# A four-layer graph kernel: adjacency tiles fetched up to 16 uses ahead, x in another queue, layer 2 counted before it is weighed, layer 3's side chains spread between its operations

## The chip, the cores and the metric

The kernel runs on one core of one Trainium2 chip. The metric is the device time in microseconds (us). Most executions of a kernel agree within about 1%. Stage times are read from one profiled execution per kernel, in microseconds from its first instruction. The granted clock of a profile is the share of its full clock that TensorE was given.

## The reference, cut to what matters

```python
# x: 3327 x 64, adj: 3327 x 3327 (sparse values in a dense float32 matrix)
h = relu(layernorm(x)); x = x + L0(h, adj)   # two gated products adj @ (h @ W)
h = relu(layernorm(x)); x = x + L1(h, adj)   # adj @ logmap0(h), then norms, tanh, projection
h = relu(layernorm(x)); x = x + L2(h, adj)   # rank of each nonzero in its row, weights 2**-k
h = relu(layernorm(x)); x = x + L3(h, adj)   # all pairs: distance, sigmoid attention * adj, sum
```

Every layer needs the whole adjacency matrix, 44 MB, and layer 0 needs it twice. It doesn't fit on the chip, so tiles are fetched again and again: 52 tiles (26 row blocks of 128 by two column groups of 12 and 14 blocks), 260 uses in a fixed order. The groups are named by their pairs of blocks: a "6-block" tile is 128x1536, a "7-block" tile 128x1792.

## The kernel before

The order of the 260 uses is known when the kernel is built. A small planner decides at build time which tile is loaded into which of the slots (16 in layers 0 and 1, 7 in layer 2, 4 in layer 3), and after which use:

```python
AHEAD = 5
...
    def ahead(self):
        for u in range(self.now, min(self.now + AHEAD, len(self.uses))):
            key = self.uses[u]
            if any(k == key and s < self.limit(u) for s, (k, _) in self.slots.items()):
                continue                      # it is there already
            wanted = set(self.uses[self.now : u + 1])
            able = [s for s, (k, _) in self.slots.items() if s < self.limit(u) and k not in wanted]
            if not able:
                break
            s = max(able, key=lambda s: self.next_use(s, self.now))   # farthest next use goes
            self.slots[s] = (key, self.load(s, key))
```

Tile loads are issued by SyncE (`nc.sync`). x, the weights and the biases are issued by ScalarE (`S`), in front of its first activation:

```python
    for ca, cb in starts:
        S.dma_start(xn[:, 2 * ca : 2 * cb, :], t["x"][:, 2 * ca : 2 * cb, :])
    ...
    # for each of two gate sets: three weights, two halves each, then two biases
    G.memset(w, 0.0)
    S.dma_start(w[h * D : (h + 1) * D, :, h * D : (h + 1) * D], ...)
    S.dma_start(b[:, 0, :], t["bih" + n])
    S.dma_start(b[:, 1, :], t["bhh" + n])
```

Work that isn't the main stream of an engine (gates, norms, the preparation of the next layer) is written as generators. `weave.tick()` lets each of them go on by one step, `weave.until(g)` runs one to its end. The order of the built instructions follows from where the ticks stand. Every engine executes its own list in that order.

Layer 2, per tile: VectorE makes a 0/1 mask, TensorE counts nonzeros with two triangular 128x128 matrices, ScalarE turns counts into weights, TensorE weighs:

```python
            mask(n + 2)
            for k in range(2):
                count(n, k)                                  # 128x128 matmuls
                flush(n, 2 if len(todo) > 2 * LAG else 1)    # weighing: 64-column matmuls
                weave.tick()
            todo += [(n, 0), (n, 1)]
```

Layer 3 is a software pipeline over 26 pairs of blocks. One iteration ends with a block of side work, and after the 13th pair a check of a bound stands in TensorE's own stream:

```python
            if n >= 0:
                gather_p(n)
                if n % HB == HB - 1:
                    collect(g)                     # evict, transpose, scale: all at once
                    final = weave.add(finish(g))
            for _ in range(6):
                weave.tick()
            if n == HB - 1:
                T.transpose(p[:2, :P], least, ident)
                V.tensor_reduce(leastr, p[:2, :P], axis=AX.X, op=OP.min)
                T.transpose(p[:1, P : P + 2], leastr, ident[:2, :2])
                ...
```

GpSimd fills three buffers of layer 3 with zeros while layer 1 ends, and the preparation of layer 3 ends with 13 small transfers that ScalarE issues, once in layer 2 and once in layer 3:

```python
    G.memset(rows_j, 0.0)          # 128 x 3328 bf16
    G.memset(rows_i, 0.0)
    G.memset(p2c, 0.0)
    ...
        for i in (6, 0, 1, 2, 3, 4, 5):
            if i == 6:
                S.dma_start(rows_l[:, ts]..., src); continue
            for lo in (0, D):
                S.dma_start(rows[r0 : r0 + 3, ts]..., src)
```

Of the kernel before, what the change touches and what calls it, by code (L numbers as in the profile page):

```python
# [43 lines left out]
AHEAD = 5  # L44
# [73 lines left out]
class Stream:  # L118
# [31 lines left out]
    def ahead(self):  # L150
        for u in range(self.now, min(self.now + AHEAD, len(self.uses))):
# [9 lines left out]
            s = max(able, key=lambda s: self.next_use(s, self.now))  # L161
            self.slots[s] = (key, self.load(s, key))

    def tile(self, key):

        assert self.uses[self.now] == key
        return next(
            a for s, (k, a) in self.slots.items() if k == key and s < self.limit(self.now)
        )
# [12 lines left out]
def gnn_kernel(ctx: ExitStack, tc: tile.TileContext, t, out):  # L182
# [27 lines left out]
    for ca, cb in starts:  # L210
        S.dma_start(xn[:, 2 * ca : 2 * cb, :], t["x"][:, 2 * ca : 2 * cb, :])
# [224 lines left out]
    def run(tg, acc, sources, m, ready, first, last):  # L436

        for i, k in enumerate(sources):
# [5 lines left out]
                stream.tile((tg, k)),  # L444
# [279 lines left out]
    def nodes3(g, m_t):  # L724
# [103 lines left out]
        yield 5  # L828
# [12 lines left out]
    with ExitStack() as c2:  # L841
# [20 lines left out]
        def mask(n):  # L862
            if n < len(work):
                a = stream.tile(work[n])
                g = GROUPS[work[n][0]]
                masks[n] = mk.tile([P, WIDE], BF16, name="mask", tag="mask", bufs=4)
                V.tensor_scalar(masks[n][:, : 2 * g.w], a, 0.0, None, op0=OP.not_equal)  # L867
                stream.done()
# [55 lines left out]
        def flush(n, most):  # L924
            while todo and most and todo[0][0] <= n - LAG:
                gens = need[work[todo[0][0]][1]]
                if weave.runs(*gens):
                    if len(todo) < 2 * (WB - 1):
# [12 lines left out]
        for n in range(len(work)):  # L941
            mask(n + 2)
            for k in range(2):
                count(n, k)
                flush(n, 2 if len(todo) > 2 * LAG else 1)
                weave.tick()
            todo += [(n, 0), (n, 1)]
        flush(len(work) + LAG, len(todo))
# [96 lines left out]
    with ExitStack() as cf:  # L1045
# [67 lines left out]
        def weights(n):  # L1113

            i, c = pairs[n]
            for b in range(2):
                a = stream.tile((i, 2 * c + b))
# [47 lines left out]
        def collect(g):  # L1165
            m = big(g, "h_n")
            m = flat(m)
# [5 lines left out]
            pp = flat(big(g, "xc"))  # L1173
# [4 lines left out]
            for p, k in each(natural(g, m)):  # L1178
                V.tensor_mul(
                    sums[:, g.slots, :D][:, k, :], p, bc(qs[:, g.slots][:, k])  # L1180
                )
            ((p, _, _),) = pieces(1)
            n0, n1 = m0 // P, m1 // P
# [9 lines left out]
            for q, n in enumerate((n0, n1)):  # L1193
# [5 lines left out]
                )  # L1199



        for n in range(-2, len(pairs)):
            if n + 2 < len(pairs) and pairs[n + 2] == (1, 0):
                weave.until(gen_s)
            if n >= 0:
                products3(n)
            if 0 <= n + 1 < len(pairs):
                distances(n + 1, 1)
            if n >= 0:  # L1210
                gather(n)
            if 0 <= n + 1 < len(pairs):
                weights(n + 1)
                squares(n + 1)
            if n + 2 < len(pairs):
                begin(n + 2)
                distances(n + 2, 0)
            if n >= 0:
                gather_p(n)
                if n % HB == HB - 1:  # L1220
                    g = GROUPS[pairs[n][0]]
                    collect(g)
                    final = weave.add(finish(g))
            for _ in range(6):
                weave.tick()
            if n == HB - 1:

                p = bank(1)
                T.transpose(p[:2, :P], least, ident)
                leastr = n3.tile([2, 1], F32, name="leastr")  # L1230
                V.tensor_reduce(leastr, p[:2, :P], axis=AX.X, op=OP.min)
                T.transpose(p[:1, P : P + 2], leastr, ident[:2, :2])
                leastr = n3.tile([1, 1], F32, name="leastr1")
                V.tensor_reduce(leastr, p[:1, P : P + 2], axis=AX.X, op=OP.min)
                within = n3.tile([1, 1], I32, name="within")
                V.tensor_scalar(within, leastr, X2_LEAST, None, op0=OP.is_ge)
            if n == HB + 1:
                ok = nc.values_load(within, min_val=0, max_val=1)
        weave.until(final)
    c3.close()  # L1240
# [223 lines left out]
```

## Time and profile before

| | before |
|---|---|
| time | 891.08 us median of 3 runs (886.57 to 892.96) |
| profiled execution | 892.6 us from the first to the last instruction |
| busy | PE 711.7 us (80%), DVE 457.2 (51%), ACT 402.8 (45%), POOL 9.7 (1%) |
| tile loads | 224, of 768 or 896 KB |

No engine is at its limit over the whole span, so the average says little. The prediction below cuts the span into stages and shows those lines. The timeline of ScalarE at the start; the columns are start, busy time, engine, line, operation, count, and in brackets the idle time before with what ended it:

```profile
32.88 1.28 ACT L468 ACT_TABLE_LOAD   x1 [32.88 <-DMA adj<-in_adj]
```

ScalarE computes nothing for 32.88 us: its list begins with transfers, and it stands behind them. Second, two timelines of layer 1's last run, VectorE and then GpSimd:

```profile
355.13 0.24 DVE L543 TENSOR_SCALAR z<-un,sc 128x14 f32<-128x14 f32 x1
356.24 0.17 DVE L633 TENSOR_SCALAR un<-un 128x14 f32<-128x14 f32 x1
```

### The profile page before, as it was taken

The numbers are of one execution on the slowest core, as the hardware profiler recorded it, in microseconds if no ns is written. First come the engines' busy times: TensorE is split into PE (matmuls) and PEld (weight loads), VectorE is DVE, ScalarE is ACT, GpSimd is POOL, SyncE is SP. The second block draws the span as 40 slices with busy tenths as digits, with TensorE's granted clock in tenths as the row PEclk, the third lists the DMA queues.
The fourth block names the chain that finished last, engine by engine and source line by source line (L and its number), as shares of the span: only waits on it lengthen the run. The fifth ranks groups of instructions, "written<-read, shape, count | busy, mean of one in ns | idle before, by whom it ended". The sixth has DMA issues, their size and how long they took to land.

```text
span 892.6 us, 10060 instructions
## 1 busy us (share of the span) xinstructions
PE 711.7 (80%) x4021; PEld 290.1 (33%) x4032; DVE 457.2 (51%) x743; ACT 402.8 (45%) x451; POOL 9.7 (1%) x20
## 2 busy tenths in 40 slices
PE   0297998989889878579998769568599995699980
PEld 0142433323334222234334324322234442244430
DVE  0230300202715402674336722488499997889976
ACT  0110200101202102176666546765599993699951
POOL 1000000000000000300000000000000000000000
PEclk9999999999999999899999979869699996799986
DMA  8819994098870999967776644123246551445600
GB/s 300 292 38 396 420 417 189 1 383 347 312 288 8 402 419 419 386 234 276 263 253 208 239 152 155 43 103 105 86 169 220 190 169 62 139 160 199 205 9 21
DMA packets 37563, 193.57 MB, mean 217 GB/s; under 512 B 7941, under 2 KB 8453, under 8 KB 37509
## 3 DMA queue, kind: packets, MB, share of 16 engines
q1 hardware_dynamic: 32544, 191.18, 56.9%
q10 hardware_dynamic: 4964, 1.68, 0.8%
q8 instruction: 33, 0.54, 0.2%
q14 instruction: 22, 0.17, 0.1%
HBM read 191.73 MB, written 0.85 MB: 216 GB/s over the span
## 4 chain that ended last, share of the span: by engine, by line
PE 51%; DMA 26%; DVE 12%; ACT 6%; issue 2%; ACTq 1%; POOL 1%; SPq 0%; DVEq 0%
DMA adj<-in_adj 23%; PE bank L428 9%; PE pair L1064 9%; PE bank L1140 9%; PE bank L916 6%; PE pair L882 4%; PE bank L1157 4%; PE pair L890 4%; PE pair L1076 2%; DVE gl L1128 1%; ACT th L1091 1%; ACT gl L1084 1%; PE pair L507 1%; PE pair L510 1%; DMA w<-in_W 1%
## 5 line engine op out<-in xcount | busy, mean ns | idle before, releaser
L428 PE MATMUL bank<-adj,m_a 128*64 128x384 f32 (+1 forms) x832 | 162.5, 527 | 25.2 <-DMA adj<-in_adj 24.4
L898 ACT ACTIVATE w<-pair,ebias 128x896 uint16<-128x896 f32 (+1 forms) x104 | 98.4, 952 | 62.1 <-PE pair L890 41.8
L1064 PE MATMUL pair<-xs 64*128 64x384 f32 x208 | 101.7, 571 | 15.7 <-ACT gl L1084 15.7
L1119 DVE SCALAR_TENSOR_TENSOR th<-th,adj 128x1792 f32<-128x1792 f32 (+1 forms) x52 | 97.8, 1886 | 21.3 <-ACT th L1091 20.9
L1084 ACT ACTIVATE gl<-pair 128x896 f32<-128x896 f32 (+1 forms) x104 | 84.1, 862 | 46.9 <-PE pair L1076 34.0
L1140 PE MATMUL bank<-gl,xd 128*64 128x384 f32 (+1 forms) x416 | 90.9, 582 | 17.3 <-DVE gl L1128 17.3
L1064 PE MATMUL pair<-xw,xs 64*128 64x384 f32 x208 | 101.4, 569 | 0.0
L1128 DVE SCALAR_TENSOR_TENSOR gl<-gl,th 128x1792 f32<-128x1792 f32 (+5 forms) x78 | 97.6, 1305 | 0.0
L428 PEld LDWEIGHTS bank<-adj,m_a 128*64 128x64 f32 x832 | 54.4, 138 | 125.7 <-DMA adj<-in_adj 65.0
L428 PE MATMUL bank<-adj,m_b 128*64 128x384 f32 (+1 forms) x416 | 81.2, 529 | 10.0 <-DMA adj<-in_adj 10.0
L1091 ACT ACTIVATE th<-leftb,righth 128x1792 f32<-128x1792 f32 (+1 forms) x52 | 87.7, 1687 | 0.0
L867 DVE TENSOR_SCALAR mask<-adj 128x1792 bf16<-128x1792 f32 (+1 forms) x52 | 52.9, 1022 | 63.5 <-PE pair L882 57.4
L421 DVE COPY m_t<-bank 128x384 f32<-128x384 f32 x6 | 3.3, 556 | 157.9 <-PE bank L428 157.9
L419 ACT ACTIVATE m_t<-bank 128x384 f32<-128x384 f32 (+1 forms) x6 | 3.3, 544 | 172.9 <-PE bank L428 172.9
L882 PE MATMUL pair<-mask,rest 128*128 128x384 bf16 (+1 forms) x190 | 65.7, 346 | 18.4 <-ACT w L898 18.3
L890 PE MATMUL pair<-mask,tri 128*128 128x384 bf16 (+1 forms) x207 | 70.7, 344 | 7.1 <-DVE mask L867 6.6
L916 PE MATMUL bank<-w,m_b 128*64 128x384 bf16 (+1 forms) x416 | 57.0, 354 | 0.0
L1140 PEld LDWEIGHTS bank<-gl,xd 128*64 128x64 f32 x416 | 33.2, 151 | 69.1 <-DVE gl L1128 37.2
L1064 PEld LDWEIGHTS pair<-xs 64*128 64x128 f32 x208 | 35.6, 197 | 43.1 <-issue 22.0
L1076 PE MATMUL pair<-rows_i,rows_j 64*128 64x384 bf16 x208 | 49.4, 353 | 0.0
L428 PEld LDWEIGHTS bank<-adj,m_b 128*64 128x64 f32 x416 | 27.7, 139 | 61.7 <-issue 32.2
L1157 PE MATMUL bank<-gl,p2c 128*32 128x384 f32 (+1 forms) x416 | 44.5, 519 | 0.0
(274 smaller groups left out, 665.1 us busy)
## 6 DMA issues: line engine op xcount, KB each, us to landing
adj<-in_adj SPq DMA_DIRECT2D x108, 896.0 KB
adj<-in_adj SPq DMA_DIRECT2D x116, 768.0 KB
xn<-in_x ACTq DMA_DIRECT2D x3, 192.0 KB
out<-h_n SPq DMA_DIRECT2D x1, 448.0 KB
out<-h_n SPq DMA_DIRECT2D x1, 384.0 KB
xn<-in_x ACTq DMA_DIRECT2D x1, 256.0 KB
ih<-in_wihT ACTq DMA_DIRECT2D x4, 48.0 KB
hh<-in_whhT ACTq DMA_DIRECT2D x4, 48.0 KB
```

Source lines behind the costliest of these rows:

```text
L428: T.matmul(acc[q][h * D : (h + 1) * D, : hi - lo], lhsT=m[:, k, :], rhs=a[:, h * g.w + lo : h * g.w + hi], start=first, stop=last,)
L882: T.matmul(dst, lhsT=rest, rhs=masks[n - 1][:, cs], start=False, stop=False, skip_group_check=True,)
L890: T.matmul(dst, lhsT=tri, rhs=masks[n][:, cs], start=first, stop=True, skip_group_check=True,)
L898: S.activation(ws[n][:, h * g.w : (h + 1) * g.w], cnt[h][:, P : P + g.w], AF.Relu, bias=ebias, scale=-EXP_UNIT,)
L916: T.matmul(acc2[i][q][h * D : (h + 1) * D, : hi - lo], lhsT=p[:, k, :], rhs=ws[n][:, h * g.w + lo : h * g.w + hi].bitcast(BF16), start=n % ...
L1064: T.matmul(pts[b][:, P + lo : P + hi], lhsT=xs[rs, c * P : (c + 1) * P], rhs=rhs[rs, g.c0 * P + lo : g.c0 * P + hi], start=True, stop=False,)
L1084: S.activation(gl[n][b][:, k * g.w : (k + 1) * g.w], pts[b][:, P : P + g.w], AF.Gelu, scale=-HA,)
L1091: S.activation(ths[n][k][:, : 2 * g.w], leftb[:, g.off : g.off + 2 * g.w], AF.Tanh, bias=righth[:, kk : kk + 1], scale=0.5,)
L1119: V.scalar_tensor_tensor(th, th, 1.0, a, op0=OP.add, op1=OP.mult)
L1128: V.scalar_tensor_tensor(a, a, hd, th[b][:, lo:hi], op0=OP.add, op1=OP.mult)
L1140: T.matmul(acc["x"][q][k * D : (k + 1) * D, : hi - lo], lhsT=xd[:, 2 * c + b, :], rhs=gl[n][b][:, k * g.w + lo : k * g.w + hi], start=firs ...
L1157: T.matmul(acc["p"][r : r + 32, : hi - lo], lhsT=p2c[:, 2 * c + b, :], rhs=a[b][:, k * g.w + lo : k * g.w + hi], start=first, stop=last,)
```

## The change

The intent: keep the transfers busy where they stood idle, bring x first, save TensorE's changes between two kinds of matmul in layer 2, and fill the idle holes of layer 3 by spreading side work. The diff, cut to its core (line numbers of the changed kernel are 2 to 4 higher):

```diff
-AHEAD = 5
+AHEAD = 16
@@ ahead()
             s = max(able, key=lambda s: self.next_use(s, self.now))
+            if self.next_use(s, self.now) < u:
+                break
             self.slots[s] = (key, self.load(s, key))
@@ x
-        S.dma_start(xn[:, 2 * ca : 2 * cb, :], ...)
+        nc.sync.dma_start(xn[:, 2 * ca : 2 * cb, :], ...)
@@ layer 2 (a tile also stays in its slot two uses longer: stream.done() moved out of mask())
-            for k in range(2):
-                count(n, k)
-                flush(n, 2 if len(todo) > 2 * LAG else 1)
-                weave.tick()
+            stream.done()
+            count(n, 0)
+            weave.tick()
+            count(n, 1)
             todo += [(n, 0), (n, 1)]
+            flush(n, 4 if len(todo) > 2 * LAG + 2 else 2)
+            weave.tick()
@@ layer 3: six single ticks, after products3, distances, weights, squares, distances and at the end
-            for _ in range(6):
-                weave.tick()
@@ layer 3: collect() split into evict() and a generator collected(), one pair later
+                if n == HB:
+                    final = weave.add(collected(gf, *evict(gf)))
@@ layer 3: the bound's check becomes a generator, started before the turn
-            if n == HB - 1:
-                ... transposes and reductions in a row ...
+                gen_b = weave.add(bound(), 4)
@@ the preparation of layer 3 waits for its rows longer
-        yield 5
+        yield 12
```

More of the change, by code (lines that the diff above doesn't have):

```diff
@@ L161, in ahead, with tile @@
             s = max(able, key=lambda s: self.next_use(s, self.now))
+            if self.next_use(s, self.now) < u:
+                break
             self.slots[s] = (key, self.load(s, key))
-    def tile(self, key):
-        assert self.uses[self.now] == key
+    def tile(self, u):
         return next(
-            a for s, (k, a) in self.slots.items() if k == key and s < self.limit(self.now)
+            a
+            for s, (k, a) in self.slots.items()
+            if k == self.uses[u] and s < self.limit(u)
         )
@@ L210, in gnn_kernel @@
     for ca, cb in starts:
-        S.dma_start(xn[:, 2 * ca : 2 * cb, :], t["x"][:, 2 * ca : 2 * cb, :])
+        nc.sync.dma_start(xn[:, 2 * ca : 2 * cb, :], t["x"][:, 2 * ca : 2 * cb, :])
     WIDE = 2 * max(g.w for g in GROUPS)
@@ L443, in run @@
                 k,
-                stream.tile((tg, k)),
+                stream.tile(stream.now),
                 m,
@@ L863, in mask @@
             if n < len(work):
-                a = stream.tile(work[n])
+                a = stream.tile(stream.starts[1] + n)
                 g = GROUPS[work[n][0]]
@@ L867, in mask @@
                 V.tensor_scalar(masks[n][:, : 2 * g.w], a, 0.0, None, op0=OP.not_equal)
-                stream.done()
         def count(n, h):
@@ L927, in flush @@
                 if weave.runs(*gens):
-                    if len(todo) < 2 * (WB - 1):
+                    if len(todo) < 2 * WB:
                         return
@@ L1116, in weights @@
             for b in range(2):
-                a = stream.tile((i, 2 * c + b))
+                a = stream.tile(stream.now)
                 th = ths[n][b][:, : 2 * GROUPS[i].w]
@@ L1163, in gather_p, with evict @@
                         )
-        def collect(g):
-            m = big(g, "h_n")
-            m = flat(m)
+        def evict(g):
+            m, pp = flat(big(g, "h_n")), flat(big(g, "xc"))
             for q, (lo, hi) in enumerate(g.chunks):
@@ L1172, in collect @@
                     V.tensor_copy(m[:, lo:hi], acc["x"][q][:, : hi - lo])
-            pp = flat(big(g, "xc"))
             m0, m1 = (hi - lo for lo, hi in g.chunks)
@@ L1177, in collect, with collected @@
                 S.activation(pp[D:, m0:m1], acc["p"][D:, m0:m1], AF.Copy)
-            for p, k in each(natural(g, m)):
-                V.tensor_mul(
-                    sums[:, g.slots, :D][:, k, :], p, bc(qs[:, g.slots][:, k])
-                )
+            return m, pp
+        def collected(g, m, pp):
+            yield
+            n0, n1 = ((hi - lo) // P for lo, hi in g.chunks)
             ((p, _, _),) = pieces(1)
-            n0, n1 = m0 // P, m1 // P
             for i in range(n1):
@@ L1199, in collect, with bound @@
                 )
+            yield
+            for p, k in each(natural(g, m)):
+                V.tensor_mul(sums[:, g.slots, :D][:, k, :], p, bc(qs[:, g.slots][:, k]))
+                yield
+            yield from finish(g)
+        def bound():
+            p = bank(1)
+            T.transpose(p[:2, :P], least, ident)
+            low = n3.tile([2, 1], F32, name="low")
+            V.tensor_reduce(low, p[:2, :P], axis=AX.X, op=OP.min)
+            yield 2
+            p = bank(1)
+            T.transpose(p[:1, :2], low, ident[:2, :2])
+            low = n3.tile([1, 1], F32, name="lowest")
+            V.tensor_reduce(low, p[:1, :2], axis=AX.X, op=OP.min)
+            V.tensor_scalar(within, low, X2_LEAST, None, op0=OP.is_ge)
+            yield
+        within = n3.tile([1, 1], I32, name="within")
+        final = None
         for n in range(-2, len(pairs)):
@@ L1205, in gnn_kernel @@
                 weave.until(gen_s)
+                gen_b = weave.add(bound(), 4)
             if n >= 0:
                 products3(n)
+                weave.tick()
+                if n == HB:
+                    final = weave.add(collected(gf, *evict(gf)))
             if 0 <= n + 1 < len(pairs):
                 distances(n + 1, 1)
+                weave.tick()
             if n >= 0:
@@ L1213, in gnn_kernel @@
                 weights(n + 1)
+                weave.tick()
                 squares(n + 1)
+                weave.tick()
             if n + 2 < len(pairs):
@@ L1217, in gnn_kernel @@
                 distances(n + 2, 0)
+                weave.tick()
             if n >= 0:
                 gather_p(n)
-                if n % HB == HB - 1:
-                    g = GROUPS[pairs[n][0]]
-                    collect(g)
-                    final = weave.add(finish(g))
-            for _ in range(6):
-                weave.tick()
-            if n == HB - 1:
-                p = bank(1)
-                T.transpose(p[:2, :P], least, ident)
-                leastr = n3.tile([2, 1], F32, name="leastr")
-                V.tensor_reduce(leastr, p[:2, :P], axis=AX.X, op=OP.min)
-                T.transpose(p[:1, P : P + 2], leastr, ident[:2, :2])
-                leastr = n3.tile([1, 1], F32, name="leastr1")
-                V.tensor_reduce(leastr, p[:1, P : P + 2], axis=AX.X, op=OP.min)
-                within = n3.tile([1, 1], I32, name="within")
-                V.tensor_scalar(within, leastr, X2_LEAST, None, op0=OP.is_ge)
+            weave.tick()
             if n == HB + 1:
+                weave.until(gen_b)
                 ok = nc.values_load(within, min_val=0, max_val=1)
         weave.until(final)
+        turn["banks"] = ()
+        for _ in collected(gs_, *evict(gs_)):
+            pass
     c3.close()
```

## The prediction

> **What bounds the kernel now.** One core, so I read the stages first, by cutting the span where the trace shows a run of tile products or a layer to begin: busy time by window. Columns: window, its length, busy microseconds and counts of PE, PEld, DVE, ACT, POOL, then the granted TensorE clock, the DMA share and GB/s.
>
> ```profile
> 0.00:41.00 41.00, 2.54 (x11) 1.91 (x11) 4.67 (x13) 4.20 (x6) 2.95 (x15) 1.00 0.82 284
> 41.00:70.70 29.70, 28.66 (x160) 13.06 (x162) 9.15 (x23) 3.44 (x9) 0.00 (x0) 1.00 0.31 120
> 70.70:147.70 77.00, 66.60 (x324) 24.45 (x322) 7.53 (x14) 5.92 (x9) 0.00 (x0) 1.00 0.96 397
> 147.70:263.20 115.50, 102.56 (x487) 38.98 (x485) 31.53 (x85) 15.33 (x25) 0.00 (x0) 0.99 0.66 257
> 263.20:370.40 107.20, 91.75 (x462) 32.92 (x458) 35.12 (x102) 18.91 (x29) 2.29 (x1) 1.00 0.76 312
> 370.40:377.00 6.60, 0.00 (x1) 0.01 (x1) 2.89 (x13) 0.49 (x1) 4.48 (x5) 0.77 0.95 393
> 377.00:561.00 184.00, 161.76 (x1084) 68.38 (x1095) 89.25 (x159) 113.40 (x133) 0.00 (x0) 0.95 0.62 218
> 561.00:655.50 94.50, 63.83 (x301) 25.46 (x299) 66.37 (x100) 62.34 (x63) 0.00 (x0) 0.78 0.29 99
> 655.50:729.90 74.40, 74.40 (x450) 31.84 (x450) 73.34 (x48) 71.45 (x65) 0.00 (x0) 1.00 0.54 189
> 729.90:790.20 60.30, 41.32 (x240) 17.72 (x239) 49.24 (x84) 36.50 (x40) 0.00 (x0) 0.80 0.34 115
> 790.20:863.50 73.30, 69.88 (x483) 32.31 (x482) 71.70 (x54) 67.78 (x69) 0.00 (x0) 0.99 0.45 152
> 863.50:892.60 29.10, 8.41 (x41) 3.07 (x41) 16.41 (x57) 3.04 (x5) 0.00 (x0) 0.62 0.04 16
> ```
>
> Rows 1 to 5 are layers 0 and 1, rows 6 and 7 layer 2, the rest layer 3. Row 3 is bound by transfers (96%), but row 2, just before it, leaves them 31% busy: the fetcher stops although the memory has work to do. The timeline and the waits say why:
>
> ```profile
> 65.58 6.78 SPq L220 DMA_DIRECT2D adj<-in_adj  x6
> 72.95 1.51 PE L428 MATMUL bank<-adj,m_a 128*64 128x384 f32 x8 [0.97 <-DMA adj<-in_adj]
> ```
> ```profile
> PEld bank L428 <- DMA adj<-in_adj: 92.8, 78, 2.4
> ```
>
> No adjacency tile is issued between 37.9 and 65.58. All 16 slots are full, but the fetcher looks only 5 uses ahead and then overwrites the tile whose next use is farthest, in this order the one just used; so the load waits for PE, and five uses later PE waits for the load.
>
> Rows 9 and 11, the steady state of layer 3, have PE, DVE and ACT all at 92 to 100%: nothing to win there. Rows 8 and 10 are holes, where side chains stand in a block:
>
> ```profile
> 631.85 1.73 ACT L1084 ACTIVATE gl<-pair 128x896 f32<-128x896 f32 x2 [12.83 <-DMA rows_j<-packt]
> 750.60 0.16 PE L1232 MATMUL bank<-ident,leastr 2*1 2x2 f32 x1 [7.97 <-DVE leastr L1231]
> ```
>
> **What the Trainium skill says.** "DMA: Bandwidth & Descriptors", section "Issuing engines are not separate DMA queues": transfers from all queues interleave on the same 16 engines. The trace agrees: ScalarE's small weight transfers take 4.6 to 8 us beside tile loads, and the windows never pass 422 GB/s. "TensorEngine Tiling (Array Packing)", section "Key Properties": a change of tiling mode, not just of tile, drains TensorE. That is layer 2's alternation of 128x128 counting and 64-column weighing, and the timeline shows it:
>
> ```profile
> 465.10 0.38 PE L882 MATMUL pair<-mask,rest 128*128 128x512 bf16 x1
> 465.31 0.38 PE L890 MATMUL pair<-mask,tri 128*128 128x512 bf16 x1
> ...
> 465.62 0.62 PE L916 MATMUL bank<-w,m_b 128*64 128x512 bf16 x4
> ```
>
> Start to start is 0.21 us within a kind and 0.31 across, so a change costs about 0.10 to 0.12. "Perfetto Trace Analysis", section "Optimizing Scalar/DVE Operations": breaking up work helps when Scalar or Vector are not saturated but cause bubbles elsewhere. Here they cause bubbles, but are saturated once the loop is steady, so spreading a chain hides its waits and not its own time.
>
> **The change, part by part.** The built order of both kernels has the same computing instructions, one more activation-table load (1.28 us in the trace) and six more loads, all of 917 KB (230 for 224, 196 MB for 190; at 420 GB/s 13 us of transfer). They replace tiles that were kept by chance.
>
> *Durations.* With tiles at hand a use takes 1.31 us for the 6-block group (64 matmuls in 10.49) and 1.53 for the 7-block group (88 in 16.76). A load takes 1.88 and 2.19 us (the issue cadence when transfers bind). Layer 0 has four runs of 26 uses (6-, 7-, 7-, 6-block), layer 1 has 14, 26 and 12.
>
> *Start.* PE begins at 41 because ScalarE's issue of weights is blocked to 32.88: each transfer waits for one of eight semaphores that tile loads also hold, for the eighth tile at the last. In the new order the last such wait is for the fourth tile, and x comes first. The two rounds of weights behind a bias transfer remain. Estimate: 3 us earlier.
>
> *Runs 1 and 2.* Loads now go out as each use ends from about 38 us on. Twenty-six of them in 7-block size and ten smaller are 75.7 us of transfer; paced by the uses of row 2 the last ends near 118. PE from use 16 needs 10 x 1.31 + 26 x 1.53 = 52.9, plus 10.1 of gate work (gaps at 95.5, 102.7, 109.9), 63 instead of 77. PE then binds, ending at 147.7 - 3 - 14 = 130.7. Gain 14.
>
> *Runs 3 and 4.* Sixteen tiles are at hand, so 36 loads (70.8 us) start with run 3 and not 12 uses later. PE: 39.8 + 34.1 + about 24.5 of gate gaps (12.3 and 12.2 in row 4) + 2 of slower clock = 100 instead of 115.5. Gain 15.
>
> *Layer 1.* 38 loads, 26 x 2.19 + 12 x 1.88 = 79.5; following the slots freed by PE, the last product ends 87 us in. PE: 18.3 + 10.6 of gate gaps + 39.8 = 68.7, then the last 12 uses. These hold the chain for layer 2 (346.1 to 368.0 in the trace, 12 uses in 23.5 us), which doesn't shrink: 92. So 92 instead of 107.2. Gain 15.
>
> *Into layer 2.* Row 6: GpSimd's fills of row buffers wait for slots that are used until the last tiles, and the first mask stands behind them. The new slot order uses these slots last some 7 tiles earlier. About 3.5 of 6.6 us remain. Gain 3.
>
> *Layer 2.* Counting both halves and then weighing has two mode changes per tile instead of four: 2 x 0.11 x 52 = 11.4 us at most; where ACT or a side chain binds (390 to 412, 505 to 523) it is lost, so 9. The 11.4 us that PE loses at 510 while ScalarE issues thirteen small transfers stay: these are untouched, and tile loads are still in flight beside them.
>
> *Layer 3.* The steady pairs take 9.36 us (7-block; 664.98 to 674.31 to 683.68 between gathers) and 8.21 us (806.65 to 814.86), and DVE's own part in them fills these times. In rows 8 and 10 the side chains have 23 and 18 us of DVE work. Row 8 holds the fill and five pairs; DVE alone needs 5 x 9.36 + 23 = 70, plus some 6 to begin and perhaps half of the 12.8 us that ScalarE is blocked: 82 to 84 for 94.5, gain about 10. Row 10 holds four pairs; 4 x 8.21 + 18 = 51, and 1 to 2 of ACT for 60.3: gain about 8. In row 12 the final chain is as long as before: 0.
>
> Sum: 3 + 14 + 15 + 15 + 3 + 9 + 18 = 77, so 891 - 77 = 814; I say 813.
>
> **Rivals.** *The transfers stay the bound*: with six loads more, deeper fetching would only shift waits. For it: 96% in row 3 and the 92.8 us of waits. Against it: rows 2 and 4 are at 31% and 66%, and in each part above the transfers end before PE or the chain. If PE ran into them everywhere, layers 0 and 1 would gain about 25 instead of 47: 835 to 840. *The chains of DVE and ACT bind once loads don't*: gates and the norm chains then stop PE at each `until`. For it: the last run of layer 1, where I took it in full. In layer 0 the chain beside run 4 ends at 247.3, 41.6 us after the run began, and run 4 needs 48. This could cost 5 to 10. *Spreading layer 3's chain does harm*: only 7 steps of it fall into the filling of the pipeline instead of 12, and a side step between two main ones makes ScalarE wait in order, with another table load. Against it: the 8 to 12 us idle gaps vanish. If it gives nothing: 831. *More than I count*: the ScalarE block may shrink with other semaphores in use, and all of layer 2's switches may pay; 795.
>
> **Range and chances.** The first five parts rest on counts and measured durations, and I give them +/-12 together; layer 2 +/-7, layer 3 +/-10. Together some +/-20, a little wider for what I overlooked: 786 to 842. A 2% gain needs only 18 of the 77 us, and no part can cost that much by itself: 96% faster, 3% the same, 1% slower.
>
> **What would show it.** Right: the second run's last product near 131, layer 1's last near 322, the weight loads' waits for tiles down from 92.8 us to under 20, no stop of loads before 65 us; layer 2 at 2.87 and 2.5 us a tile instead of 3.1 and 2.73; layer 3's fill and turn near 84 and 52 us, its steady pairs unchanged. Wrong: DMA share above 0.95 through layer 1 with PE waiting for tiles, a longer blocked ScalarE near the row transfers, or DVE idle in the fill.

## More of the kernel before

```profile
368.11 2.87 POOL L692 MEMSET rows_j<- 128x3328 bf16 x1 [338.58 <-DMA adj<-in_adj]
```

The small operations of the chain that leads to layer 2 take 0.17 to 0.24 us, and the fills come 11 us after them.

## The result, and the profile after

The changed kernel takes **835.05 us** (median of 4 runs, 833.85 to 837.84) against 892.02 us for the kernel before in the same rounds. Ratios in this document are the mean of one kernel's fast runs over the mean of the other's fast runs of the same rounds, so they aren't quite the ratio of the quoted medians; here 0.9373, 95% interval 0.9322 to 0.9424. It is faster, and 22 us slower than predicted.

The profiled execution took 832.0 us with a granted clock of 0.951. Busy time by window, cut at much the same events as in the prediction (from layer 3's fill on at the weights of the sixth, 14th and 18th pair, up to 2 us from the prediction's cuts; the columns are as there; rows 1 to 3, 5, 7, 8 and 10 of twelve):

```profile
0.00:44.50 44.50, 2.50 (x9) 1.86 (x9) 4.60 (x13) 4.20 (x6) 2.94 (x15) 1.00 0.77 257
44.50:74.30 29.80, 28.74 (x160) 13.11 (x162) 9.22 (x23) 3.45 (x9) 0.00 (x0) 1.00 0.99 401
74.30:136.90 62.60, 62.36 (x326) 26.30 (x324) 7.53 (x14) 5.91 (x9) 0.00 (x0) 1.00 0.87 358
...
235.40:330.60 95.20, 87.30 (x460) 35.88 (x456) 39.86 (x102) 18.90 (x29) 6.75 (x5) 0.98 0.94 377
...
332.90:509.50 176.60, 152.56 (x1097) 75.97 (x1097) 89.26 (x159) 109.14 (x133) 0.00 (x0) 0.95 0.69 243
509.50:600.90 91.40, 62.24 (x302) 26.08 (x302) 66.10 (x99) 64.35 (x64) 0.00 (x0) 0.83 0.29 102
...
678.70:731.90 53.20, 39.06 (x236) 17.38 (x235) 47.46 (x81) 38.30 (x41) 0.00 (x0) 0.90 0.37 127
```

Row 2 has a DMA share of 0.99 where it was 0.31. Row 3 is the stage that waited for tiles: PE is now busy 62.36 of 62.60 us. The waits of the weight loads for tiles, the groups with the time in all, the count and the longest, and the issues of SyncE's queue say the same:

```profile
PEld bank L431 <- DMA adj<-in_adj: 11.8, 25, 1.2
```

```profile
35.05 44.76 SPq L223 DMA_DIRECT2D adj<-in_adj  x26
```

The 92.8 us of waits are 11.8, and the loads go on through the stretch from 37.9 to 65.58 us in which none was issued before.

The stages against the prediction, all from the two profiled executions (gain positive). The "turn" is where layer 3 goes over from its first 13 pairs to the second 13:

| stage | before | after | gain | predicted |
|---|---|---|---|---|
| to the first product | 41.0 | 44.5 | -3.5 | 3 |
| layer 0, runs 1 and 2 | 106.9 | 92.4 | 14.5 | 14 |
| layer 0, runs 3 and 4 | 115.5 | 98.5 | 17.0 | 15 |
| layer 1 | 107.0 | 95.2 | 11.8 | 15 |
| into layer 2 | 6.6 | 2.3 | 4.3 | 3 |
| layer 2 | 184.2 | 176.6 | 7.6 | 9 |
| layer 3, fill and five pairs | 95.0 | 91.4 | 3.6 | 10 |
| layer 3, eight steady pairs | 75.5 | 77.8 | -2.3 | 0 |
| layer 3, turn | 59.5 | 53.2 | 6.3 | 8 |
| layer 3, rest and tail | 101.4 | 100.1 | 1.3 | 0 |
| sum | 892.6 | 832.0 | 60.6 | 77 |

Sixteen us of the gain are missing in the spans. (The other six of the 22: the span of the profiled execution of before lies 1.5 us above the median from which the prediction started, that of after 3 us below its median, and 1 us of the prediction's own rounding.) Most is missing in four stages: the start, layer 1, the fill, and the pairs that follow the fill. The lines for them, each a timeline: ScalarE at the start, ScalarE in layers 2 and 3, then GpSimd and VectorE in layer 1's last run.

```profile
36.45 1.28 ACT L471 ACT_TABLE_LOAD   x1 [36.45 <-DMA b_l<-in_L2b]
```

```profile
470.04 1.69 ACT L900 ACTIVATE w<-pair,ebias 128x768 uint16<-128x768 f32 x2 [13.49 <-DMA rows_j<-packt]
...
582.27 1.79 ACT L1111 ACTIVATE gl<-gl,hg 128x1792 f32<-128x1792 f32 x1 [10.70 <-DMA rows_j<-packt]
```

```profile
310.90 2.88 POOL L695 MEMSET rows_j<- 128x3328 bf16 x1 [277.74 <-PE bank L431]
313.73 2.89 POOL L696 MEMSET rows_i<- 128x3328 bf16 x1
```

```profile
311.01 2.80 DVE L546 TENSOR_SCALAR z<-un,sc 128x14 f32<-128x14 f32 x1
...
314.40 0.17 DVE L634 TENSOR_TENSOR th<-th,e 128x14 f32<-128x14 f32 x1
...
314.70 1.96 DVE L636 TENSOR_SCALAR un<-un 128x14 f32<-128x14 f32 x1
```

ScalarE starts 3.6 us later. It is stopped twice by the row transfers, for 13.49 and 10.70 us. In layer 1 the two operations that took 0.24 and 0.17 us take 2.80 and 1.96; the first ends at 313.81, just after the first fill (313.78), the second at 316.66, just after the second (316.62). The two-input operations between them keep their 0.17 us.

In layer 2 the order on TensorE is now one block of counting and one of weighing per tile:

```profile
415.68 0.38 PE L884 MATMUL pair<-mask,rest 128*128 128x512 bf16 x1
415.89 0.38 PE L892 MATMUL pair<-mask,tri 128*128 128x512 bf16 x1
416.20 0.52 PE L918 MATMUL bank<-w,m_b 128*64 128x384 bf16 x4
```

The change of kind costs as much as before (415.89 to 416.20, 0.31 us start to start against 0.21 within a kind); there are half as many. A tile takes 2.88 us (7-block) and 2.50 (6-block), where it took 3.1 and 2.73.

### The profile page after: what moved, and what is told of

The parts are those of the page before. It is cut to its first block, busy times and chain, and to the rows that moved or that the text cites. A ratio compares the mean times of both kernels' runs of the same rounds, so it can differ in the third digit from the quotient of the medians.

```text
span 832.0 us, 10106 instructions
## 1 busy us (share of the span) xinstructions
PE 682.1 (82%) x4032; PEld 303.2 (36%) x4032; DVE 460.1 (55%) x742; ACT 399.7 (48%) x452; POOL 9.7 (1%) x20
## 5 line engine op out<-in xcount | busy, mean ns | idle before, releaser
L431 PE MATMUL bank<-adj,m_a 128*64 128x384 f32 (+1 forms) x832 | 153.1, 523 | 3.1 <-DMA adj<-in_adj 2.4
L900 ACT ACTIVATE w<-pair,ebias 128x896 uint16<-128x896 f32 (+1 forms) x104 | 94.4, 949 | 54.6 <-PE pair L892 40.8
L1068 PE MATMUL pair<-xs 64*128 64x384 f32 x208 | 101.4, 569 | 0.9 <-ACT gl L1088 0.9
L1088 ACT ACTIVATE gl<-pair 128x896 f32<-128x896 f32 (+1 forms) x104 | 84.0, 862 | 25.7 <-PE pair L1080 25.6
L1144 PE MATMUL bank<-gl,xd 128*64 128x384 f32 (+1 forms) x416 | 85.9, 550 | 9.8 <-DVE gl L1132 8.6
L431 PEld LDWEIGHTS bank<-adj,m_a 128*64 128x64 f32 x832 | 58.6, 139 | 90.1 <-issue 78.1
L884 PE MATMUL pair<-mask,rest 128*128 128x384 bf16 x200 | 69.2, 347 | 21.9 <-ACT w L900 21.9
L431 PE MATMUL bank<-adj,m_b 128*64 128x384 f32 (+1 forms) x416 | 74.1, 514 | 0.0
L892 PE MATMUL pair<-mask,tri 128*128 128x384 bf16 x208 | 70.9, 345 | 2.3 <-DVE mask L870 2.3
L1068 PEld LDWEIGHTS pair<-xw,xs 64*128 64x128 f32 x208 | 35.4, 195 | 47.0 <-ACT gl L1088 43.4
L1111 ACT ACTIVATE gl<-gl,hg 128x1792 f32<-128x1792 f32 (+1 forms) x26 | 43.7, 1681 | 10.7 <-DMA rows_j<-packt 10.7
```

Of the source, the lines that this page charges most:

```text
L431: T.matmul(acc[q][h * D : (h + 1) * D, : hi - lo], lhsT=m[:, k, :], rhs=a[:, h * g.w + lo : h * g.w + hi], start=first, stop=last,)
L884: T.matmul(dst, lhsT=rest, rhs=masks[n - 1][:, cs], start=False, stop=False, skip_group_check=True,)
L892: T.matmul(dst, lhsT=tri, rhs=masks[n][:, cs], start=first, stop=True, skip_group_check=True,)
L900: S.activation(ws[n][:, h * g.w : (h + 1) * g.w], cnt[h][:, P : P + g.w], AF.Relu, bias=ebias, scale=-EXP_UNIT,)
L1068: T.matmul(pts[b][:, P + lo : P + hi], lhsT=xs[rs, c * P : (c + 1) * P], rhs=rhs[rs, g.c0 * P + lo : g.c0 * P + hi], start=True, stop=False,)
L1088: S.activation(gl[n][b][:, k * g.w : (k + 1) * g.w], pts[b][:, P : P + g.w], AF.Gelu, scale=-HA,)
```

## The experiments

All twelve gave correct results, and all ran three rounds beside the kernel before. "Fill" is the stretch from layer 2's last weighing to the weights of the sixth pair (91.4 us in the changed kernel), "turn" that from the weights of the 14th pair to those of the 18th (53.2). Kernels with the same layer 3 show how well such stretches repeat: the fill is 91.4 to 93.6 in five of them, the turn 53.2 to 54.9.

### The fetching rule alone

The kernel before, with only this:

```diff
-AHEAD = 5
+AHEAD = 16
+            if self.next_use(s, self.now) < u:
+                break
```

> The kernel before with the fetching rule alone: 16 uses ahead, and no tile thrown out that is used sooner than the one fetched. Theory: the rule is the whole gain of the stages before layer 2 and gives nothing after it; first product near 41, end of run 2 near 134, layer 1's end near 328, layer 2 at the old pace of 3.1 and 2.73 us a tile, layer 3 as before; about 848 us, ratio 0.95. Rival: the gain of layer 2 comes from earlier loads too (its tiles are there sooner), then the time is about 840 and layer 2 takes 177 instead of 184 us. If the collision of fills and chain at layer 1's end comes with the new rule, its last run takes 27 us here, if it comes from the layer 3 part of the change, 23.5.

Measured: 848.11 us (844.88 to 849.91), ratio 0.9521 (0.9476 to 0.9565). First product at 40.7, end of run 2 at 133.3, end of layer 1 at 328.2 us. From the first matmul of layer 2 to layer 3's first weights it took 193.4 us (194.4 before, 183.1 in the changed kernel); turn 59.5 and rest as before. So the rule alone is three quarters of the gain: 43 of the 57 us by the medians. Everything before layer 2 is its work, and nothing after. The two long operations of layer 1 are here too (2.84 and 2.80 us at 307.19 and 310.07), so they come with the rule and not with the change in layer 3 (the last 13 uses of layer 1 take 30.2 us here, 25.7 before): slots are free earlier, so GpSimd fills the buffers that lie in them earlier, beside the chain.

### x back in ScalarE's queue

```diff
-        nc.sync.dma_start(xn[:, 2 * ca : 2 * cb, :], ...)
+        S.dma_start(xn[:, 2 * ca : 2 * cb, :], ...)
```

> The changed kernel with x fetched through ScalarE's queue again. Theory A: the 11 more first loads take the semaphores that the queues share, so ScalarE's small transfers wait longer wherever x goes: first product at 44 to 46, time 835 to 838. Theory B: moving x itself made the start late: first product back at 41, time about 831. Theory C, that of the prediction: x first gains 3 us, so it is lost here: first product at 47 or later and 838 or more.

Measured: 834.22 us (831.85 to 834.99), ratio 0.9356 (0.9319 to 0.9393). The first product is at 41.5 us, ScalarE's first work at 33.42. Theory B holds for the start: moving x made it late, not the 11 more loads.

```profile
33.42 1.28 ACT L471 ACT_TABLE_LOAD   x1 [33.42 <-DMA w_l<-in_L2w]
```

The other kernels agree, though the start differs from kernel to kernel: with x in ScalarE's queue the first product is at 40.7 to 41.5 us (three kernels), with x in SyncE's and the weights still in ScalarE's at 42.3 to 46.7 (eight). At the end the 3 us can't be told from the run-to-run difference. The sign of this step of the prediction was wrong: x landed 3 us earlier (3.17 instead of 6.2 us), but ScalarE doesn't wait for x alone. It stands behind all its weights and biases, and in the new order the biases of the second set were issued at 26.70 and 28.02 us instead of 23.19 and 23.83.

### The weights through GpSimd's queue

```diff
-            S.dma_start(w[h * D : (h + 1) * D, :, h * D : (h + 1) * D], ...)
+            G.dma_start(w[h * D : (h + 1) * D, :, h * D : (h + 1) * D], ...)
```

and likewise the biases and the constants of the start, 22 transfers in all.

> The changed kernel with the weights and biases of the start issued by GpSimd instead of ScalarE. Theory: ScalarE's first activation waits at 37.7 us only because its queue stands behind these transfers; without them it starts once x has come, the first product is at 12 to 28 us instead of 44.5, and most of it reaches the end: 815 to 822 us. Rival: the loads of the tiles bound run 1 and 2 then (16 tiles have landed by about 34 us only), and the end of run 2 moves from 136.9 by less than 5 us: 831. Rival 2: the weights land no earlier through GpSimd, so the first product stays after 40 us.

Measured: 821.86 us (819.91 to 826.8), ratio 0.9226 (0.9192 to 0.9261), 13 us less than the changed kernel. Busy time by window:

```profile
0.00:11.40 11.40, 2.49 (x9) 1.86 (x9) 4.62 (x13) 4.20 (x6) 6.46 (x17) 1.00 0.81 249
11.40:47.00 35.60, 29.30 (x158) 11.92 (x158) 9.36 (x23) 3.56 (x9) 9.88 (x20) 1.00 1.00 382
47.00:122.80 75.80, 67.02 (x328) 24.80 (x328) 7.53 (x14) 5.91 (x9) 0.00 (x0) 1.00 0.94 387
```

The first product is at 11.4 us, 33 us earlier, so it was ScalarE's queue that held the start. At the end of run 2 only 14 of the 33 are left (122.8 for 136.9): with a DMA share of 1.00 and 0.94 the loads bind these stages now. The theory holds for the start and for the time. The first rival holds in part: the loads take 19 of the 33 us, but the end of run 2 moves by 14 us and not by less than 5. One more rival stands untested. By the semaphore numbers in the packed traces the transfers of ScalarE and SyncE take turns on eight semaphores, and those of GpSimd on eight others, so this edit may also free the tile loads: in its trace the 16th is issued at 26.8 us, where it was at 41.8. How much of the 13 us comes from ScalarE's list and how much from the earlier loads, no run here takes apart.

### The row transfers through GpSimd's queue

```diff
-                S.dma_start(rows_l[:, ts]..., src)
+                G.dma_start(rows_l[:, ts]..., src)
-                S.dma_start(rows[r0 : r0 + 3, ts]..., src)
+                G.dma_start(rows[r0 : r0 + 3, ts]..., src)
```

> The changed kernel with the row transfers of layer 3's preparation issued by GpSimd, which is idle, instead of ScalarE. Theory: ScalarE's stop of 11 us in layer 2 and in layer 3's fill is time in which it stands blocked behind transfers that it issues; without it layer 2 takes 167 instead of 176.5 us and the first part of layer 3 (to the weights of its sixth pair) 84 instead of 91; about 819 us. Rival: the rows' landing is what the fill waits for, then layer 2 gains, layer 3's fill nothing, 826. Rival 2: layer 2 makes it good elsewhere, 835.

Measured: 809.42 us (808.22 to 810.73), ratio 0.9083 (0.9047 to 0.9119), 25.6 us less than the changed kernel and more than the theory's 16. Busy time of layer 2 and of the fill:

```profile
336.50:498.50 162.00, 149.92 (x1097) 75.15 (x1097) 89.39 (x159) 109.04 (x133) 10.16 (x13) 0.99 0.75 263
498.50:576.70 78.20, 58.93 (x300) 25.59 (x302) 65.77 (x99) 64.21 (x64) 7.45 (x13) 0.85 0.35 119
```

Layer 2 takes 162.0 instead of 176.6 us, the fill 78.2 instead of 91.4. ACT has the same work in both (109.04 for 109.14, 64.21 for 64.35). Both rivals fall: it isn't the landing of the rows that the fill waits for, it is ScalarE standing in its own list, and layer 2 doesn't make it good elsewhere. Both stops cost all of their length, 14.6 for 13.49 and 13.2 for 10.70. The excess isn't taken apart; in part TensorE ran faster: it has the same work in layer 2, but 149.92 us of it for 152.56, at a granted clock of 0.99 for 0.95.

### Layer 2's order back

```diff
-            count(n, 0)
-            weave.tick()
-            count(n, 1)
+            for k in range(2):
+                count(n, k)
+                flush(n, 2 if len(todo) > 2 * LAG else 1)
+                weave.tick()
             todo += [(n, 0), (n, 1)]
-            flush(n, 4 if len(todo) > 2 * LAG + 2 else 2)
-            weave.tick()
...                                  # a limit in flush() goes back too: 2 * (WB - 1)
```

> The changed kernel with layer 2's order of before: count a half, weigh what is due, count the other half. Theory: two of the four mode changes a tile come back, 0.1 us each; layer 2 at 3.1 and 2.73 us a tile instead of 2.88 and 2.50, and about 8 to 10 us longer: 844. Rival: the order hardly matters and the pace of layer 2 came with the earlier loads; then the pace stays and the time is 835. The run with the fetching rule alone (layer 2's stretch 193.4 us, as in the kernel before) speaks for the theory.

Measured: 844.36 us (841.34 to 845.76), ratio 0.9461 (0.9434 to 0.9489): 9.3 us more by the medians. The timeline shows four changes a tile again:

```profile
422.11 0.50 PE L892 MATMUL pair<-mask,tri 128*128 128x384 bf16 x2
422.54 0.52 PE L918 MATMUL bank<-w,m_b 128*64 128x384 bf16 x4
...
423.15 0.50 PE L892 MATMUL pair<-mask,tri 128*128 128x384 bf16 x2
```

Counting, weighing and counting again within 1.04 us. Layer 2 is 6.9 us longer (183.5 for 176.6, first matmul at 333.7, last weighing at 517.2), and some 2 us of the rest show in the fill (93.6; the other four kernels with this layer 3 have 91.4 to 92.4). The theory holds, and its size too.

### Layer 3's side chains in blocks again, without and with the row transfers moved

```diff
@@ the loop over the pairs
                 products3(n)
-                weave.tick()
...                                  # the other four single ticks go too
-            weave.tick()
+            for _ in range(6):
+                weave.tick()
@@ nodes3
-        yield 12
+        yield 5
```

> The changed kernel with layer 3's side chains in blocks of six steps at the end of an iteration, as before. By the step of the prediction the fill is 10 and the turn 8 us longer: 853. By what the run with the fetching rule alone showed (from the first to the fourteenth pair's weights 160.8 us, against 162.7 in the changed kernel) the fill is not longer at all, only the turn by about 6: 838 to 841. If the block only moved where the waiting is and the turn's gain came from the bound's check being moved away, 835.

Measured: 834.4 us (831.88 to 835.96), ratio 0.9351 (0.9329 to 0.9374): no difference to the changed kernel. The fill is 94.5 us (3.1 longer, and 0.9 longer than the longest of the equal ones), but the steady pairs are 77.0 (0.8 shorter), the turn 52.2 (1.0 shorter) and the tail 1.2 shorter. What spreading wins in the fill it gives back over the rest of the layer.

The second kernel has the same edit and the row transfers in GpSimd's queue:

> Layer 3's side chains in blocks at the end of an iteration, with the row transfers issued by GpSimd. Rival to what the run with the blocks alone says: spreading the chains pays, but ScalarE's stop hid it, since both orders had to wait for it; then this run is 6 to 10 us longer than the run with the rows moved alone (809.4): 815 to 820, with its first part of layer 3 (weights of the first pair to those of the sixth) near 80 instead of 71.8 us. Theory: spreading is worth nothing in the fill: 808 to 811, that part 71 to 73.

Measured: 812.71 us (811.15 to 813.26), ratio 0.9096 (0.9046 to 0.9146). That lies between the two expectations. The stretch from the first pair's weights to the sixth's is 74.4, nearer to the theory, but counted from layer 2's last weighing the fill is 84.5 us against 78.2. So with ScalarE free, spreading is worth 6.3 us in the fill, and with ScalarE stopped only 3.1: the stop hid half of it. Some 3 us of the 6 reach the end (812.71 for 809.42), which these rounds can't hold apart from none.

### The bound's check back, without and with the blocks

```diff
-                gen_b = weave.add(bound(), 4)
@@ at the end of the 13th pair's iteration
+            if n == HB - 1:
+                T.transpose(p[:2, :P], least, ident)
+                V.tensor_reduce(low, p[:2, :P], axis=AX.X, op=OP.min)
+                T.transpose(p[:1, P : P + 2], low, ident[:2, :2])
+                V.tensor_reduce(low, p[:1, P : P + 2], axis=AX.X, op=OP.min)
+                V.tensor_scalar(within, low, X2_LEAST, None, op0=OP.is_ge)
```

> The changed kernel with the bound's check of before: both of its transposes and reductions in a row after the thirteenth pair, in TensorE's own order, with no other work between. Theory: the turn's gain came from moving this check, not from spreading; TensorE waits some 8 us for VectorE there again, the stretch from the fourteenth to the eighteenth pair's weights is 59 instead of 53.2 us, 841. Rival: the gain is that of the spread chains; then the stretch stays at 53 to 55, 835 to 836.

Measured: 835.5 us (833.59 to 837.52), ratio 0.9355 (0.9301 to 0.9408). My theory falls. The check's own wait and the longest wait of TensorE near it (timeline) are

```profile
684.24 0.16 PE L1257 MATMUL bank<-ident,low 2*1 2x2 f32 x1 [0.37 <-DVE low L1256]
...
688.68 4.27 PE L1144 MATMUL bank<-gl,xd 128*64 128x384 f32 x16 [2.47 <-DVE h_n L1175]
```

0.37 and 2.47 us, no 7.97, and the turn is 55.3. The last experiment has check and blocks together:

> Both at once: the side chains in blocks of six steps at the end of an iteration, and the bound's check of before directly behind the block of the thirteenth pair. Each alone left the turn (weights of the fourteenth pair to those of the eighteenth) at 52.2 and 55.3 us. Theory: the 7.97 us that TensorE waited came from the check standing behind a whole block of side work on VectorE, so it takes both, and the turn is 58 to 60 us here, 838 to 842. Rival: the turn's gain came from the third part, the sums that are now collected in steps one pair later; this run keeps that part, so the turn stays at 52 to 55 and the time at 834 to 836.

Measured: 836.98 us (836.26 to 837.88), ratio 0.9384 (0.932 to 0.9449). The turn is 55.8 us, so this theory falls too. The only part of the turn's change that is left in this kernel is the split collection of the sums, and 3.7 of the 6.3 us (59.5 to 55.8) stay with it; that is by subtraction, it wasn't run alone. The check's own wait is 0.37 us here too, so the 7.97 us seem to have needed the collection all at once. The check costs 3.7 us with blocks (52.2 to 55.8) and 2.1 without (53.2 to 55.3), the latter about what equal kernels differ by. Spreading is worth nothing in the turn.

This run also shows, by single profiles, what made the eight steady pairs longer. They take 75.0 us here, as before the change (75.5), where the changed kernel takes 77.8, the one with blocks alone 77.0 and the one with the check alone 77.4: the spread steps and the check's new place cost the 2.3 us together.

### The fills in small pieces

```diff
-    G.memset(rows_j, 0.0)
-    G.memset(rows_i, 0.0)
+    for r in (rows_j, rows_i):
+        for i in range(13):
+            G.memset(r[:, 256 * i : 256 * i + 256], 0.0)
```

> The changed kernel with GpSimd's two fills of 128x3328 cut into 13 pieces of 128x256 each (0.2 to 0.3 us by size). Theory: a VectorE operation that falls beside a fill stands until that one GpSimd instruction ends; with small pieces no operation of the chain in layer 1's last run takes over 0.6 us where two took 2.80 and 1.96, the last 13 uses take 25 to 26 us instead of 28.9, and the time is about 831 to 832. Rival: GpSimd keeps the port from one piece to the next and the chain loses the same 4.5 us; 835. Rival 2: the two long operations have nothing to do with the fills; then they stay at the same places with the same times.

Measured: 829.9 us (826.31 to 835.02), ratio 0.9319 (0.9273 to 0.9366). The last 13 uses take 23.6 us instead of 28.9 (another 2 us of this profile's gain are an earlier start, 42.3 for 44.5, which the edit doesn't touch). The longest operation of the small ones is (timeline of VectorE):

```profile
310.06 0.41 DVE L636 TENSOR_SCALAR un<-un 128x14 f32<-128x14 f32 x1
```

That looked like the theory. But the next kernel, which has the same pieces, refutes it.

### Rows, weights and small pieces together

The edits of three experiments above in one kernel.

> The changed kernel with row transfers and start weights issued by GpSimd and the fills in 13 pieces each. The gains lie in different stages, so they should add: 25.6 (rows) + 13.2 (start) + 3 to 4 (fills) from 835: 792 to 795, ratio 0.89. Rival: with an earlier start the loads bind further on, and the earlier layers lose a part: 800.

Measured: 794.27 us (789.5 to 795.89), ratio 0.8896 (0.886 to 0.8932). The two large gains add up as expected. The gain of the fills doesn't: the last 13 uses take 31.0 us, and the same operation on VectorE shows why:

```profile
298.91 6.10 DVE L636 TENSOR_SCALAR un<-un 128x14 f32<-128x14 f32 x1
```

It stands for 6.10 us, to 305.01; the 26 pieces end at 304.10 and the third fill, unsplit, at 304.84. So a VectorE operation that meets the fills may wait for a whole row of GpSimd instructions and not only for the one under way. (That the fills are the cause, the next run shows; how they keep it out so long is inferred from the times.) In the run before it waited 0.24 us. Cutting a fill into pieces is no protection.

### Rows and weights moved, fills by VectorE itself

```diff
-    G.memset(rows_j, 0.0)
-    G.memset(rows_i, 0.0)
-    G.memset(p2c, 0.0)
@@ nodes3, the chain in layer 2 that needs the buffers
+        if g is gf:
+            for r in (rows_j, rows_i, p2c):
+                V.memset(r, 0.0)
+                yield
```

> Rows and start weights through GpSimd's queue as in the run that had both and took 794.3 us; but the three fills are done by VectorE in layer 2, at the head of the chain that needs them, and not by GpSimd at all. Theory: with no fill beside it the chain of layer 1's last run has no operation of 2 us or more (there was one of 6.10), its last 13 uses take 23.6 to 25 us instead of 31.0, and VectorE has room for the fills in layer 2: about 787. Rival: the 6.10 us were something else, and the stretch stays near 31: 794. Rival 2: in layer 2 the fills delay the chain that leads to the rows by 3 us or more: 790.

Measured: **789.48 us** (788.6 to 790.56), ratio 0.8839 (0.8791 to 0.8887). The last 13 uses take 23.0 us, no small operation there is slow, and the fills take VectorE 1.45, 1.45 and 0.75 us in layer 2 (163.5 us instead of 162.3 in the run with GpSimd's pieces). Of the 8 us won in layer 1 some 5 arrive: layer 2 takes 1.3 back, the fill 0.8 and the turn 1.7, the last two no more than equal kernels differ by. The time lies between the theory (787) and the second rival (790). This is the best version: 45.6 us faster than the changed kernel, 103 faster than before.

## Why the prediction was right or wrong

The verdict (faster by over 2%), the range and the order of the parts were right. The time was 22 us too low. By the steps of the prediction:

- **Start ("3 us earlier").** Wrong in sign, 6.5 us off. The failed step is that waits for tiles hold ScalarE's list ("for the eighth tile at the last") and that x first and fewer such waits therefore bring the start forward. I took the name at the one long wait in the profile before for its cause. By the semaphore numbers and landing times in the packed traces, the last of these transfers that waited for a tile went out at 13.87 us before and at 13.96 after; the eighth tile had landed 5.7 us before the transfer behind it in turn went out (25.76 and 31.44). The two rounds behind a bias transfer, which the prediction let stand, set the start. They end (GpSimd's first use of the biases) at 18.99 and 29.19 us before, at 20.15 and 32.83 after, because the second biases now stand behind their own set's first two weight transfers, which land 6.2 and 6.9 us after their issue (3.6 and 3.3 before). Why these land later isn't settled. (The prediction's "4.6 to 8 us" for small weight transfers is too narrow, too: those of its trace land in 2.8 to 8.1.) The run with x back starts at 41.5, so it is the move of x that delays; the run with the weights on GpSimd starts at 11.4, so it is the position of 22 transfers in ScalarE's list, and no landing of x, that sets the start.
- **Runs 1 and 2 (14), runs 3 and 4 (15).** Right: 14.5 and 17. The rule alone gives both. The waits for tiles fell from 92.8 to 11.8 us; loads are issued through the hole.
- **Layer 1 (15).** 11.8. The failed step is that the chain of its last run "doesn't shrink": it grew. The chain meets GpSimd's fills, which the new fetching rule lets run earlier. The prediction saw that the fills would run earlier and took it as pure gain ("into layer 2", 3 us, got 4.3). The Trainium skill, "SBUF — State Buffer", section "Who interferes with whom", says that a VectorE operation in a two-port mode and a GpSimd operation block each other, and that single-input copies and tensor-scalar operations can enter such a mode, while two-input operations contend only with a GpSimd operation that reads. This trace agrees: beside the fills, which only write, tensor-scalar operations took 2.80 and 1.96 us and tensor-tensor ones their usual 0.17. With the fills taken off GpSimd the stretch is 23.0 us instead of 28.9; before the change it was 25.7.
- **Layer 2 (9).** Right: 7.6 here, 9.3 by undoing it. The 11.4 us for which TensorE stops "stay", as predicted (11.8), and the row experiment shows their worth: 14.6.
- **Fill (10).** The mechanism was right, a size was off: 3.6. The mis-sized term is "perhaps half of the 12.8 us that ScalarE is blocked". Without the stop the fill takes 78.2 us, close to the 76 that the prediction had without it (70 of VectorE and 6 to begin); with it 91.4. So the stop costs 13.2 us and not 6.4. The prediction took it as overlapping with VectorE's work; but VectorE's main work there needs what ScalarE makes, and it stood 9.06 us for ScalarE's first activation behind the stop. This also hid half of what spreading won (3.1 us instead of 6.3).
- **Pairs after the fill (0).** 2.3 us worse. All of it goes when blocks and check both come back (75.0), 0.8 and 0.4 when one of them does: the prediction counted nothing for the side work that moves into them.
- **Turn (8).** 6.3, for another reason than I gave, so the number came near by luck. The reason was that spreading fills the idle holes. Blocks give the same turn (52.2). What is left points to the split collection, about 4, and the moved check, 2 to 4, of which some 2 are lost again in the pairs before. Two theories of mine on the 7.97 us wait fell before that. Over the whole of layer 3, from layer 2's last weighing to the end, it is 331.3 us before, 327.2 with the split collection alone of its three parts, 322.5 with the moved check as well, and 322.4 with spreading too.
- **Tail (0).** 1.3, about what equal kernels differ by (100.1 to 101.0 in eight of them).

Of the rivals, "spreading layer 3's chain does harm" came nearest: spreading gives no gain at the end, as the run with blocks shows, though for the fill alone it helps. "The transfers stay the bound" was wrong in this kernel, and became true of runs 1 and 2 once the start was moved forward by 33 us. "The chains bind once loads don't" came true in layer 1's last run, where TensorE waits 4.44 us for the chain's end.

## What to carry to other kernels

A load planner that looks ahead only a few uses can leave the memory idle while all slots are full; look for a stretch without issues next to a stretch at full transfer rate. Before an engine is found idle "for a transfer", see whether it waits for the data or only stands behind its own issues: moving twice 13 and 22 small transfers to an idle engine's queue was worth 26 and 13 us here, together as much as two thirds of the planned change (with the open question of the semaphores for the 13). And a part of the program that becomes free earlier will start earlier: ask what it then runs beside.

## What the Trainium skill lacked or had wrong

- "DMA: Bandwidth & Descriptors", section "Issuing engines are not separate DMA queues", says that issuing from several engines saves only the time that a sequencer takes to issue, usually small beside the transfer. One issue is small here too: 0.72 us (median) for a row transfer that lands in 2.0 to 8.6 us. What the page doesn't weigh is the issuing engine's own work: 13 such issues in a row are some 9.4 of the 13.49 us for which ScalarE couldn't compute, and taking them off it (twice) saved 25.6 us.
- "SBUF — State Buffer", section "Who interferes with whom", says that the loser is blocked for the whole instruction of the other engine. The runs show two cases: a wait that ended with the one fill under way (2.80 us, ending 0.03 after it), and, with the fills in 26 pieces of about 0.3 us, one of 6.10 us that outlasted some 20 pieces and the fill behind them. In another run with the same pieces the same operation took 0.41 us. The page doesn't say that a row of GpSimd instructions can keep VectorE out.
- No page that I found says what moving a transfer to another queue does to transfers that stay: x moved out of ScalarE's queue made ScalarE's first work 3 us later (33.42 to 36.45 us).
